# P6 of the feed-forward residual by leaves in the first two blocks, and an engine order picked from 800 plans

## The chip, the cores and the metric

The kernel runs on one core of one Trainium2 chip. The metric is the device time of one execution in microseconds (us); lower is better. Before the change the median of three runs is 566.54 us (566.49 to 567.19).

## The reference

The input is x of 2 x 2048 rows of 512 float32 numbers, and a condition of 2 x 512. What is computed, cut to what matters here:

```python
emb = jnp.dot(jax.nn.silu(t), ada_w) + ada_b
shift_msa, scale_msa, gate_msa, shift_mlp, scale_mlp, gate_mlp = jnp.split(emb, 6, axis=-1)
norm = _ln(x) * (1.0 + scale_msa[:, None]) + shift_msa[:, None]
h = jax.nn.gelu(jnp.dot(norm, ssm_w1) + ssm_b1, approximate=False)
x = x + gate_msa[:, None] * (jnp.dot(h, ssm_w2) + ssm_b2)
norm2 = _ln(x) * (1.0 + scale_mlp[:, None]) + shift_mlp[:, None]
hf = jax.nn.gelu(jnp.dot(norm2, ff_w1) + ff_b1, approximate=True)
x = x + gate_mlp[:, None] * (jnp.dot(hf, ff_w2) + ff_b2)
```

ssm_w1 and ssm_w2 are 512 x 512, ff_w1 is 512 x 1024 and ff_w2 is 1024 x 512. Everything is float32.

## The kernel before, in words

The 4096 rows are cut into eight blocks of 512 rows. Blocks 0 to 3 belong to the first batch entry, 4 to 7 to the second. First comes the part that the code calls ssm: for each block `norm1`, `ssm1` (the product with ssm_w1 and the gelu), `ssm2` (the product with ssm_w2, gated, added to x) and `norm2`. Then comes the feed-forward part in four steps s of two blocks each: `ff1(s)` makes the hidden layer of two blocks, and `ff2(s, 0)` and `ff2(s, 1)` the two outputs.

**Products by seven parts.** No product is done plainly. Each is split into 2 x 2 quarters and made of seven products of sums (the scheme of Strassen and Winograd; the code calls them P1 to P7). `first` (line 420) and `second` (line 430) make the sums of the quarters by elementwise adds, and the seven products are collected in the accumulating banks of PSUM, in the order that lets one bank carry a partial sum on to the next part. Most products are split twice: a part that is itself made of seven smaller ones is done "by leaves". A leaf has half the columns of a plain part.

**ff2.** For one block, `ff2` (line 1114) forms the operands of the seven outer parts from the hidden layer with `first`, then splits P1, P2, P3, P4, P5 and P7 once more, also with `first`. `chain(r)` for r from 0 to 4 does the leaves of P1, P5 and P7, each in a bank of its own; `parts_of(r)` for r from 0 to 6 does those of P2, P3 and P4 and adds them into the rows of the block; `gather` adds a finished bank to the rows. P6 comes last of the outer parts, and there are two forms of it. `plain_sixth` does it unsplit: 8 matmuls of 256 columns in round 4. `sixth` does it by leaves: 14 matmuls of 128 columns spread over the rounds 0 to 4, with four copies on ScalarE, two adds on GpSimd (POOL) and two adds on VectorE into the bank of P1. Which form is used depends on whether the weights hold leaves for P6 (`by_leaves = "P6" in wops`, line 1179). `fw2_sixth` (line 934) makes these leaves of the weights with four adds of 128 x 256. The main program calls it at the start of the step s = 1 (line 1437), so blocks 0 and 1 use `plain_sixth` and blocks 2 to 7 use `sixth`; for the second batch entry it is called right after the weights are loaded.

**What sets the order.** The code first records every operation in `Plan` (line 21) with its engine or engines, its expected cost and latency, and what it depends on. TensorE's operations run in the order in which they were recorded. For the others, `order` (line 88) sets a latest start for each, counted back from the time at which TensorE is due to need the result, and `simulate` (line 111) plays all engines through and always picks, on each free engine, the most urgent operation that is ready. An elementwise add that has all its operands in SBUF can go to VectorE or to POOL. The simulation also chooses which, and lets only one of the two engines work on such adds at a time. Every DMA but a few goes through SP's queue, and eight are in flight at most. The two rounds of `order` differ only in that the second moves the due times by how late TensorE began at one fixed operation (`anchor`, the first matmul of `ssm1(0)`). The operations are then issued in the order of their planned starts, and each engine keeps that order on the chip and waits by semaphores.

Where the prediction speaks of lines: 256 is `tt`, the elementwise add, subtraction or product of two tensors; 274 an activation; 283 a copy on ScalarE; 294 a matmul; 304 a transpose on TensorE; 316 a DMA; 522 and 523 the statistics of a normalization; 591 the transpose on VectorE in it. The names of tiles are those of SBUF regions that hold several things in turn: `rows` is where ff2 adds up its output (and x in ssm), `hidden` holds the hidden layer, `near` and `far` the sums for ff2, `fw` the weights of ff2, `ring` the loaded parts of ff_w1 and sums for ff1, `turned` the normalized and transposed rows; `bank` is PSUM.

Of the kernel before, what the change touches and what calls it, by code (L numbers as in the profile page):

```python
# [1 line left out]

# [12 lines left out]


class Op:
    __slots__ = ("n", "engs", "fn", "cost", "lat", "shared", "size", "lead", "care", "after", "done", "sooner", "deps", "succ", "late", "on", "start", "end", "note")


class Plan:
# [11 lines left out]
    LITTLE = 1 << 15  # L33
    LANES = 8
    AHEAD, SLACK = 2500.0, 150.0

    def __init__(self, nc):
        self.nc = nc
        self.engines = {"p": nc.tensor, "v": nc.vector, "a": nc.scalar, "g": nc.gpsimd, "s": nc.sync}
        self.ops, self.wrote, self.read, self.known = [], {}, {}, {}  # L40
        self.stage, self.care = "", 0.0
# [44 lines left out]
        return op  # L86

    def order(self):
        ops = self.ops
        for op in ops:  # L90
            if op.engs == "p":
                op.deps = {d for d in op.deps if ops[d].engs != "p"}
            for d in op.deps:
                ops[d].succ.append(op.n)
        t, due = 0.0, {}
        for op in ops:
            if op.engs == "p":
                due[op.n] = t
                t += op.cost["p"]
        for _ in range(2):  # L100
            for op in reversed(ops):
                late = due.get(op.n, 1e9)
                for s in op.succ:
                    late = min(late, ops[s].late - (1 + op.care) * (self.HOP + min(op.lat.values()) + op.size / self.RATE))
                op.late = late - op.sooner
            self.simulate()
            wait = ops[self.anchor].start - due[self.anchor]
            due = {n: t + wait for n, t in due.items()}
        return sorted(ops, key=lambda op: (op.start, op.n))

    def simulate(self):
        ops, hop = self.ops, self.HOP
# [86 lines left out]
def kernel(  # L199
# [51 lines left out]
    def tt(e, o, a, b, f):  # L251
        n, ps = cols(o), in_psum(a, b)
        cost = {"v": n / 0.96 + 70, "g": 2.12 * n + 145}
        plan.add(
            e,
            lambda E: E.tensor_tensor(o, a, b, f),  # L256
            [o],
            [a, b],
            cost,
            {"v": cost["v"] + 85, "g": cost["g"] + 45},  # L260
            "g" if ps else "vg",
        )
# [90 lines left out]
    for n in range(8):  # L353
        t = psum.tile([P, 2 * HT], F32, tag=f"bank{n}", name=f"bank{n}")
# [143 lines left out]
    def gate(g, b, bank):  # L498
        if (g, b) == (2, 0):
            return first_gate(bank)  # L500
        load_row(gate_sb, gates_d[g][b])
        if bank is None:
            return gate_sb
        copy(banks[bank], gate_sb)
        return banks[bank]

    def gate_bias(t, g_ps, row):
        load_row(t, row)
        tt("v", t, g_ps, t, ALU.mult)
        tt("vg", t[:, D // 2 :], t[:, D // 2 :], t[:, : D // 2], ALU.subtract)  # L510
# [364 lines left out]
    def quarter_row(b):  # L875
        t = cut(gb2[b], "p (h e d) -> p h e d", h=2, e=2)
        tt("vg", t[:, :, 1], t[:, :, 1], t[:, :, 0], ALU.subtract)

    def weight2(b, bank):
        plan.stage = f"weight2 {b}"  # L880
        t = w2_t[b]
        load_w(t, w2)
        g = gate(2, b, bank)
        gate_bias(gb2[b], g, b2)
        for k in range(KD):
            tt("v", t[:, k, :], t[:, k, :], g, ALU.mult)
        return second(quarters_of_second(t, KD), thirds(w2_s), cuts=1)
# [45 lines left out]

    def fw2_sixth(plain, leaves):
        leaves["P6"] = leaves_of(plain, 6)

    def weight_fw2(b, bank):
        plan.stage = f"weight_fw2 {b}"
        for n in range(2):
            for o in range(2):  # L940
                dma(fw2_t[:, 4 * n + 2 * o : 4 * n + 2 * o + 2], fw2_source()[n, o], lead=100000.0)
        g = gate(5, b, bank)
        gate_bias(gb5, g, fb2)
        for n in range(2):
# [472 lines left out]
    for i in range(1, NBLK):  # L1417
        if i + 3 < NBLK:
            plan.care = 0.45
            tok[i + 3] = norm1(i + 3)  # L1420
            plan.care = 0.45
        last = i + 2 >= NBLK
        hooks = second_head(i + 1, hid[i + 1]) if last and i + 1 < NBLK else {}
        ssm2(i, hid[i], w2_ops, CARRIED, hooks)
        if i in SOON:
            norm2(i)
        if i == 4:
            ff = weight_fw2(0, 1)
        if i + 1 == PER_B:
            w2_ops = weight2(1, 1)  # L1430
            quarter_row(1)
            w2_leaves[0] = second_leaves(w2_ops)
        if not last:
            hid[i + 2] = ssm1(i + 2, tok[i + 2], w1_ops, second_head(i + 1, hid[i + 1]))
    for s in range(NBLK // 2):
        if s == 1:
            fw2_sixth(*ff)
        if 2 * s == PER_B:
            ff = weight_fw2_loaded(1)
            fw2_sixth(*ff)  # L1440
        if 2 * s + 2 == PER_B:
            weight_fw2_ahead(1)
        ff1(s)
        if 2 * s + 2 < NBLK and 2 * s + 2 not in SOON:
            normed2(2 * s + 2)
        for blk in range(2):
            ff2(s, blk, *ff)
# [51 lines left out]
```

## Time and profile before

| | before |
|---|---|
| median of 3 runs | 566.54 us |
| the profiled execution | 566.59 us |
| its span, first to last instruction | 564.8 us |
| TensorE busy (PE) | 557.8 us, 99% |
| VectorE busy (DVE) | 483.1 us, 86% |
| POOL busy | 379.0 us, 67% |
| ScalarE busy (ACT) | 266.0 us, 47% |
| granted TensorE clock | 1.00 |
| HBM | 209 GB/s over the span |

How to read it: PE is TensorE's matmuls and PEld its weight loads, which run beside them. A matmul of float32 leaves two records in the trace, and a record's time includes the way through the array, so that records overlap: a long row of records is read by the distance of their starts. A group's row ends with the idle time of the engine just before its instructions, and with what ended it. A timeline row is: start, length from the first start to the last end, engine, line, operation, output <- inputs, shape, how many; in brackets the idle time ahead of it and who ended it.

### The profile page before, as it was taken

The numbers are of one execution on the slowest core, as the hardware profiler recorded it, in microseconds if no ns is written. First come the engines' busy times: TensorE is split into PE (matmuls) and PEld (weight loads), VectorE is DVE, ScalarE is ACT, GpSimd is POOL, SyncE is SP. The second block draws the span as 40 slices with busy tenths as digits, with TensorE's granted clock in tenths as the row PEclk, the third lists the DMA queues.
The fourth block names the chain that finished last, engine by engine and source line by source line (L and its number), as shares of the span: only waits on it lengthen the run. The fifth ranks groups of instructions, "written<-read, shape, count | busy, mean of one in ns | idle before, by whom it ended". The sixth has DMA issues, their size and how long they took to land.

```text
span 564.8 us, 10322 instructions
## 1 busy us (share of the span) xinstructions
PE 557.8 (99%) x3553; PEld 506.3 (90%) x3553; DVE 483.1 (86%) x918; ACT 266.0 (47%) x534; POOL 379.0 (67%) x514
## 2 busy tenths in 40 slices
PE   8999999999999999999999999999999999999997
PEld 4888889888898988889999889999889999888997
DVE  5696978888879989898989899999999888789776
ACT  3473856674888845557102347212366122336120
POOL 2887638979826687995547866776776784446660
PEclk9999999999999999999999999999999999999999
DMA  8953799989799879895047899078956041820022
GB/s 315 398 221 87 233 343 308 316 240 320 223 268 369 257 271 273 273 323 185 4 147 255 302 286 332 18 204 282 321 172 198 2 151 46 272 95 28 1 75 74
DMA packets 53057, 119.85 MB, mean 212 GB/s; under 512 B 5473, under 2 KB 10509, under 8 KB 51470
## 3 DMA queue, kind: packets, MB, share of 16 engines
q1 hardware_dynamic: 51842, 118.66, 63.9%
q8 instruction: 28, 0.46, 0.3%
q10 hardware_dynamic: 1164, 0.55, 0.3%
q14 instruction: 23, 0.19, 0.1%
HBM read 77.63 MB, written 40.51 MB: 209 GB/s over the span
## 4 chain that ended last, share of the span: by engine, by line
PE 94%; DVE 3%; DMA 1%; issue 1%; POOL 0%; SPq 0%; DVEq 0%
PE bank L294 94%; DMA fw<-in_L_cond_ada_w_dram 1%; DVE hidden L256 1%; DVE near L256 0%; DVE marks L522 0%; PE bank L304 0%; POOL hidden L256 0%; POOL near L256 0%; SPq L316 0%; DVE rows L256 0%; DVE ring L256 0%; DVE fw L256 0%; DVE far L591 0%; DVE turned L656 0%; DVE marks L523 0%
## 5 line engine op out<-in xcount | busy, mean ns | idle before, releaser
L294 PE MATMUL bank<-turned,ring 128*128 128x256 f32 x896 | 208.7, 380 | 0.2 <-DVE turned L656 0.2
L294 PEld LDWEIGHTS bank<-turned,ring 128*128 128x128 f32 x896 | 167.6, 190 | 22.9 <-DVE turned L656 0.5
L256 DVE TENSOR_TENSOR hidden<-bank,hidden 128x512 f32<-128x512 f32 (+1 forms) x171 | 125.2, 755 | 28.0 <-PE bank L294 24.8
L294 PE MATMUL bank<-near,hidden 128*128 128x256 f32 (+1 forms) x470 | 95.3, 350 | 0.3 <-DVE rows L256 0.2
L294 PEld LDWEIGHTS bank<-near,hidden 128*128 128x128 f32 x470 | 82.1, 190 | 10.0 <-DVE rows L256 0.6
L294 PE MATMUL bank<-fw,hidden 128*128 128x128 f32 x640 | 90.4, 275 | 0.0
L256 DVE TENSOR_TENSOR rows<-bank,rows 128x128 f32<-128x128 f32 (+3 forms) x154 | 78.8, 554 | 11.4 <-PE bank L294 10.9
L294 PE MATMUL bank<-ring 128*128 128x256 f32 x336 | 82.4, 381 | 0.5 <-DVE hidden L256 0.5
L294 PEld LDWEIGHTS bank<-fw,hidden 128*128 128x128 f32 x640 | 81.2, 192 | 0.4
L283 ACT COPY bank<-bank 128x512 f32<-128x512 f32 (+2 forms) x88 | 37.3, 425 | 83.3 <-PE bank L294 82.2
L256 POOL TENSOR_TENSOR turned<-turned 128x512 f32<-128x512 f32 (+1 forms) x56 | 63.1, 1139 | 16.7 <-ACT turned L274 9.4
L294 PEld LDWEIGHTS bank<-ring 128*128 128x128 f32 x336 | 63.2, 190 | 11.2 <-issue 1.7
L294 PE MATMUL bank<-fw,far 128*128 128x128 f32 (+2 forms) x644 | 67.6, 278 | 0.7 <-DMA fw<-in_L_cond_ada_w_dram 0.7
L294 PEld LDWEIGHTS bank<-fw,far 128*128 128x128 f32 (+1 forms) x644 | 60.9, 167 | 2.7 <-issue 1.7
L274 ACT ACTIVATE hidden<-hidden,cols 128x512 f32<-128x512 f32 (+1 forms) x66 | 45.0, 712 | 37.9 <-DVE hidden L256 37.8
L294 PE MATMUL bank<-fw,near 128*128 128x128 f32 (+1 forms) x452 | 61.1, 279 | 0.0
L256 POOL TENSOR_TENSOR hidden<-hidden 128x128 f32<-128x128 f32 (+2 forms) x52 | 43.6, 847 | 22.6 <-DVE hidden L256 6.4
L294 PEld LDWEIGHTS bank<-fw,near 128*128 128x128 f32 x452 | 56.0, 192 | 0.4
L256 POOL TENSOR_TENSOR fw<-fw 128x256 f32<-128x256 f32 (+1 forms) x52 | 45.0, 875 | 13.3 <-DVE fw L256 7.7
L274 ACT ACTIVATE turned<-turned,mod,mod 128x512 f32<-128x512 f32 x56 | 41.5, 805 | 8.2 <-DMA turned<-turned 7.2
L256 POOL TENSOR_TENSOR ring<-turned,ring 128x256 f32<-128x256 f32 x37 | 27.8, 757 | 15.8 <-PE bank L294 9.7
L256 DVE TENSOR_TENSOR hidden<-hidden 128x512 f32<-128x512 f32 (+2 forms) x58 | 34.9, 621 | 1.2 <-ACT hidden L274 0.8
(136 smaller groups left out, 692.4 us busy)
## 6 DMA issues: line engine op xcount, KB each, us to landing
ring<-fw_parts SPq DMA_DIRECT2D x28, 512.0 KB
turned<-far SPq DMA_DIRECT2D x52, 256.0 KB
ring<-fw_parts SPq DMA_DIRECT2D x28, 384.0 KB
rows<-x SPq DMA_DIRECT2D x32, 256.0 KB
turned<-turned SPq DMA_DIRECT2D x32, 256.0 KB
out_dram<-rows SPq DMA_DIRECT2D x28, 256.0 KB
fw_parts<-fw SPq DMA_DIRECT2D x21, 256.0 KB
fw<-in_L_cond_ada_w_dram SPq DMA_DIRECT2D x5, 1024.0 KB
```

Of the source, the lines that this page charges most:

```text
L256: lambda E: E.tensor_tensor(o, a, b, f),
L274: lambda E: E.activation(o, a, func, bias=bias, scale=scale),
L283: plan.add("a", lambda E: E.copy(o, a), [o], [a], {"a": cost}, {"a": cost + 60})
L294: lambda E: E.matmul(o, lhsT, rhs, start=start, stop=stop, skip_group_check=True, **kw),
```

## The change

Two things change. First, `fw2_sixth` is called right after `weight_fw2(0, 1)` (after block 4 of ssm2), not at s = 1. So the weights hold P6's leaves from the start, and blocks 0 and 1 use `sixth` as the others do.

Second, `order` no longer takes the one plan. It draws up 800 more with a fixed seed. Each takes the last accepted plan, picks a gap of over 30 ns that TensorE has in it (the longer, the likelier), goes back from an operation that the gap waited for over a few of its predecessors, and asks for that operation earlier by 0.5 to 3 times the gap (`wanted`). `draw_up` sets the latest starts with these wishes and runs `simulate`. The plan's cost is then the end of TensorE in `follow`, which plays the order that came out, unchanged, in three cases: with 700 ns to land for a transfer at the full rate, with 2200 ns, and with 1200 ns at 0.85 of the rate. A plan that costs a little more is accepted too, less and less so; the cheapest of all is issued.

```diff
-        t, due = 0.0, {}
-        for op in ops:
-            if op.engs == "p":
-                due[op.n] = t
-                t += op.cost["p"]
-        for _ in range(2):
-            for op in reversed(ops):
-                late = due.get(op.n, 1e9)
-                for s in op.succ:
-                    late = min(late, ops[s].late - (1 + op.care) * (self.HOP + min(op.lat.values()) + op.size / self.RATE))
-                op.late = late - op.sooner
-            self.simulate()
-            wait = ops[self.anchor].start - due[self.anchor]
-            due = {n: t + wait for n, t in due.items()}
-        return sorted(ops, key=lambda op: (op.start, op.n))
+        tensor = [op for op in ops if op.engs == "p"]
...
+        draw = random.Random(2)
+        wanted, (cost, gaps) = {}, self.draw_up({})
+        best = cost, wanted
+        for n in range(self.ROUNDS):
+            other = dict(wanted)
+            if other and draw.random() < 0.3:
+                del other[draw.choice(list(other))]
+            for d, over in draw.choices(gaps, [g[0] for g in gaps])[0][1]:
+                for _ in range(draw.choice((0, 0, 1, 2, 3, 5, 8))):
+                    before = [u for u in ops[d].deps if ops[u].engs != "p"]
+                    if not before:
+                        break
+                    d = max(before, key=lambda u: ops[u].end)
+                other[d] = other.get(d, 0.0) + over * draw.choice((0.5, 1.0, 1.5, 3.0))
+            found = self.draw_up(other)
+            if found[0] <= cost + draw.random() * self.WARMTH * (1 - n / self.ROUNDS):
+                wanted, (cost, gaps) = other, found
+                if cost < best[0]:
+                    best = cost, wanted
+        self.draw_up(best[1])
+        return self.sequence
...
+    def follow(self, landing, pace, gaps):
...
+        for op in self.sequence:
...
+            if e == "p" and start > free[e] + self.LEAST and op.n > self.anchor:
+                gaps.append((start - free[e], [(d, end[d] + hop - free[e]) for d in op.deps if end[d] + hop > free[e]]))
+            free[e] = start + op.cost[e]
+        return free["p"]
...
         if i == 4:
             ff = weight_fw2(0, 1)
+            fw2_sixth(*ff)
...
     for s in range(NBLK // 2):
-        if s == 1:
-            fw2_sixth(*ff)
         if 2 * s == PER_B:
```

More of the change, by code (lines that the diff above doesn't have):

```diff
@@ L1 @@
+import random
 from contextlib import ExitStack
@@ L17 @@
 class Op:
-    __slots__ = ("n", "engs", "fn", "cost", "lat", "shared", "size", "lead", "care", "after", "done", "sooner", "deps", "succ", "late", "on", "start", "end", "note")
+    __slots__ = ("n", "engs", "fn", "cost", "lat", "shared", "size", "lead", "care", "after", "done", "sooner", "deps", "succ", "due", "late", "on", "start", "end", "note")
 class Plan:
@@ L35 @@
     AHEAD, SLACK = 2500.0, 150.0
+    ROUNDS, WARMTH, LEAST = 800, 300.0, 30.0
+    CASES = ((700.0, 1.0), (2200.0, 1.0), (1200.0, 0.85))
     def __init__(self, nc):
@@ L109, in order @@
-        return sorted(ops, key=lambda op: (op.start, op.n))
+        tensor = [op for op in ops if op.engs == "p"]
+        t = 0.0
+        for op in tensor:
+            op.due, t = t, t + op.cost["p"]
+        self.draw_up({})
+        wait = ops[self.anchor].start - ops[self.anchor].due
+        for op in tensor:
+            op.due += wait
+        draw = random.Random(2)
[17 more added lines that the diff above has]
+                    best = cost, wanted
@@ new lines, in order, with draw_up @@
+        self.draw_up(best[1])
+        return self.sequence
+    def draw_up(self, wanted):
+        ops = self.ops
+        for op in reversed(ops):
+            late = op.due if op.engs == "p" else 1e9
+            for s in op.succ:
+                late = min(late, ops[s].late - (1 + op.care) * (self.HOP + min(op.lat.values()) + op.size / self.RATE))
+            op.late = late - op.sooner - wanted.get(op.n, 0.0)
+        self.simulate()
+        self.sequence = sorted(ops, key=lambda op: (op.start, op.n))
+        cost, gaps = 0.0, []
+        for landing, pace in self.CASES:
+            cost += self.follow(landing, pace, gaps) / len(self.CASES)
+        return cost, gaps
@@ new lines, in follow @@
+    def follow(self, landing, pace, gaps):
+        ops, hop, end = self.ops, self.HOP, [0.0] * len(self.ops)
+        free = dict.fromkeys("pvags", 0.0)
+        pipe, lock, lanes = 0.0, 0.0, [0.0] * self.LANES
+        for op in self.sequence:
+            e = op.on
+            ready = 0.0
+            for d in op.deps:
+                t = end[d] if ops[d].on == e and not ops[d].size else end[d] + hop
+                if t > ready:
+                    ready = t
+            start = max(free[e], ready)
+            if op.size:
+                start = max(start, lanes[0])
+                pipe = max(start + self.FLIGHT, pipe) + op.size / (self.RATE * pace)
+                end[op.n] = (pipe if op.size > self.LITTLE else start + op.lat[e]) + landing
+                lanes = lanes[1:] + [end[op.n]]
+            else:
+                if e in op.shared:
+                    start = max(start, lock)
+                    lock = start + op.cost[e]
+                end[op.n] = start + op.lat[e]
+            if e == "p" and start > free[e] + self.LEAST and op.n > self.anchor:
+                gaps.append((start - free[e], [(d, end[d] + hop - free[e]) for d in op.deps if end[d] + hop > free[e]]))
+            free[e] = start + op.cost[e]
+        return free["p"]
```

## The prediction

> **What bounds the kernel now.** I read the page's first and fourth parts, then the busy times by stage, then the chain of waits, and last the timeline at each place where TensorE stands still.
>
> ```profile
> span 564.8 us, 10322 instructions
> ...
> PE 557.8 (99%) x3553; PEld 506.3 (90%) x3553; DVE 483.1 (86%) x918; ACT 266.0 (47%) x534; POOL 379.0 (67%) x514
> ...
> PE 94%; DVE 3%; DMA 1%; issue 1%; POOL 0%; SPq 0%; DVEq 0%
> ```
>
> TensorE is busy for 557.8 of 564.8 us and makes up 94% of the chain, so only two things can shorten the run: less work on TensorE, and the few waits that are left. The profiled execution took 566.59 us, 1.8 more than its span and 0.05 more than the median of the three runs (566.54).
>
> ```profile
> core 0: us, PE busy (x) PEld busy (x) DVE busy (x) ACT busy (x) POOL busy (x), PEclk, DMA share, GB/s
> ...
> 33.10:208.17 175.07, 174.81 (x989) 155.69 (x989) 147.01 (x307) 120.45 (x243) 123.96 (x214) 1.00 0.82 265
> ...
> 255.36:342.68 87.32, 87.08 (x565) 80.68 (x565) 79.13 (x141) 28.95 (x59) 57.07 (x60) 1.00 0.60 204
> 342.68:429.34 86.66, 86.65 (x588) 80.84 (x589) 81.64 (x144) 34.89 (x73) 61.86 (x68) 1.00 0.64 209
> 429.34:515.91 86.57, 86.56 (x588) 80.82 (x589) 74.13 (x130) 29.47 (x64) 51.96 (x56) 1.00 0.38 119
> ```
>
> The columns are the stretch, its length, and what each engine is busy of it. I cut at the end of each feed-forward up-projection (ff1), so each of the last three rows holds two blocks of ff2 and the next ff1. The second row is blocks 0 and 1, which do P6 plainly; the third is blocks 2 and 3, which do it by leaves, and it is 0.66 us shorter. The first row, the bulk of ssm, has TensorE busy for all but 0.26 us. The granted clock is 1.00 in all, so no throttle enters the sum.
>
> **Part 1: P6 by leaves in blocks 0 and 1.** Per block, `plain_sixth` is 8 matmuls of 256 columns, and `sixth` is 14 of 128. A float32 matmul leaves two records here: the two groups below hold 2 blocks x 8 matmuls in 32 records. Behind them stands the timeline of narrow ones.
>
> ```profile
> L294 PE MATMUL bank<-fw,near 128*128 128x256 f32 x16 | 3.6, 379 | 0.0
> L294 PE MATMUL bank<-fw,far 128*128 128x256 f32 x16 | 3.6, 379 | 0.0
> ```
>
> ```profile
> 384.26 1.06 PE L294 MATMUL bank<-fw,hidden 128*128 128x128 f32 x8
> 385.15 0.61 PE L294 MATMUL bank<-fw,far 128*128 128x128 f32 x4
> 385.60 1.27 PE L294 MATMUL bank<-fw,hidden 128*128 128x128 f32 x8
> ```
>
> Records overlap, so the spacing counts. Sixteen wide ones take 3.6 us and the last is 0.38 long: (3.6 - 0.38) / 15 = 0.215. Eight narrow ones run from 384.26 to 385.15: 0.111 to 0.112. So 16 x 0.216 = 3.46 us becomes 28 x 0.112 = 3.14: 0.32 less per block, **-0.64** for two. The stretches agree: 0.66 apart, with almost the same waits in both.
>
> The other instructions of this part lie beside TensorE. Per block there are three adds of 128x256 for the leaves, one subtraction, four copies on ScalarE (29 of 87 us busy), two small adds on POOL and two adds into the bank on VectorE. At 0.41 us an add that is at most 3.7 us more on VectorE in that stretch (nine such adds, four or five per block). VectorE then has 82.8 of about 86.7 us, hardly more than the 81.6 of 86.66 that blocks 2 and 3 show with the same work. The four adds that make P6's leaves of the weights leave ff2 1 and go into `weight_fw2 0`, where one of them is on POOL. They lie in the first row's stretch, where TensorE hardly waits, so I cost them at nothing; if that cover went, their price would be 4 x 0.41 = 1.6 at most.
>
> **Part 2: the order.** TensorE keeps its order; what moves is VectorE, POOL, ScalarE and SP between 26 us and the end. So I go from one stop of TensorE to the next, with the instruction order of both programs beside it.
>
> The stop at 207.9 us (last block of ssm2):
>
> ```profile
> 203.45 4.48 PE L294 MATMUL bank<-near,hidden 128*128 128x256 f32 x20
> ...
> 206.86 0.68 DVE L591 STREAM_TRANSPOSE far<-near 128x512 f32<-128x512 f32 x1
> ...
> 207.46 0.65 DVE L256 TENSOR_TENSOR rows<-bank,rows 128x512 f32<-128x512 f32 x1
> ...
> 208.17 1.35 PE L294 MATMUL bank<-near,hidden 128*128 128x256 f32 x5 [0.24 <-DVE rows L256]
> ```
>
> Twenty records at 0.216 make the next due at 207.77; it starts at 208.17, 0.40 late, and the five records then take 1.35 instead of 4 x 0.216 + 0.38 = 1.24, so 0.10 is lost in starting again: 0.50 in all. It waits for the `rows` add, which stands behind a transpose that nobody needs yet. In the new order this add stands ahead of that transpose. It then starts at 206.86 and ends at 207.51, 0.26 before it is needed: **-0.50**. Late next is the transpose, by one add; only the normalization of a later block waits for it. The `rows` add after it moves ahead of a transpose as well, so no stop takes the place of this one.
>
> The stops at the ends of ff1 0 and ff1 1:
>
> ```profile
> 252.80 2.32 PE L294 MATMUL bank<-turned,ring 128*128 128x256 f32 x10
> 255.36 1.10 PE L294 MATMUL bank<-ring 128*128 128x256 f32 x4 [0.24 <-DVE hidden L256]
> ...
> 339.68 2.75 PE L294 MATMUL bank<-turned,ring 128*128 128x256 f32 x12
> 342.68 1.10 PE L294 MATMUL bank<-ring 128*128 128x256 f32 x4 [0.24 <-DVE hidden L256]
> ...
> 426.56 2.77 PE L294 MATMUL bank<-turned,ring 128*128 128x256 f32 x12
> 429.34 1.10 PE L294 MATMUL bank<-ring 128*128 128x256 f32 x4
> ```
>
> By the same reckoning the first is due at 254.96 and comes at 255.36 (0.40 late, 0.07 for the new start), the second is 0.41 + 0.07 late, but the third, the end of ff1 2, only 0.19 + 0.07. The arithmetic is the same in all three. In the first two the last adds on VectorE stand as wide (128x1024), narrow (128x512), narrow, wide, narrow, and TensorE waits for the last. In ff1 2 one narrow add stands elsewhere: wide, narrow, wide, narrow. The new order has this form in ff1 0 and ff1 1 too. So each goes from 0.47 to about 0.26: **-0.44** in all. What stays is the last narrow add itself, which waits for the matmul ahead of it.
>
> A new stop, early in block 1 of ff2. In the old order the adds that make P7 and its leaves for block 1 stand before ff2 0's last two wide adds on VectorE; in the new one two adds of 128x512 and the 128x256 add that needs them stand behind the second wide one.
>
> ```profile
> 278.06 1.06 PE L294 MATMUL bank<-fw,hidden 128*128 128x128 f32 x8
> ...
> 278.21 1.23 DVE L256 TENSOR_TENSOR rows<-bank,rows 128x1024 f32<-128x1024 f32 x1
> ```
>
> The three adds as groups of that stretch (busy, mean ns of one), and two neighbours on the timeline:
>
> ```profile
> L256 DVE TENSOR_TENSOR near<-near 128x512 f32<-128x512 f32 x3 | 2.1, 684 | 0.1
> L256 DVE TENSOR_TENSOR fw<-fw 128x256 f32<-128x256 f32 x3 | 1.2, 411 | 0.0
> ```
>
> ```profile
> 255.13 0.68 DVE L256 TENSOR_TENSOR near<-near 128x512 f32<-128x512 f32 x1
> 255.73 0.69 DVE L256 TENSOR_TENSOR hidden<-hidden 128x512 f32<-128x512 f32 x1
> ```
>
> On the old clock the wide add starts at 278.21. End to end the four take 1.23 + 0.68 + 0.68 + 0.41 = 3.00. Neighbours overlap by 0.08 (the two rows at 255), so 2.76 is the least, and 0.2 for the step between an add and one that needs it is the most that I allow over 3.00. So the leaf is ready between 280.97 and 281.4. TensorE gets there after 24 narrow records from 278.06, at 280.75. The wait is 0.2 to 0.65, with 0.1 for the new start: **+0.3 to +0.75, and I take +0.5**, because POOL holds the same two-input adds there. It is the price of a plan that puts three leaf adds more on this stretch.
>
> At 28 us two gating products of weight2 change places on VectorE, so TensorE can be held one step earlier.
>
> ```profile
> 30.54 1.29 POOL hidden L256
> 31.83 1.25 POOL near L256
> 33.08 0.04 issue
> 33.12 3.72 PE bank L294 x16
> ```
>
> The chain of waits above (start, length, what) shows that this costs nothing: TensorE starts at 33.12 because a POOL chain ends then, and that chain stays as it was.
>
> One more stop is lost time of another kind: in the row at 385.60 eight records take 1.27 where eight took 1.06, so 0.21 is lost. VectorE was late, and these rows of VectorE and POOL show why:
>
> ```profile
> 382.86 2.04 DVE L256 TENSOR_TENSOR turned<-turned 128x512 f32<-128x512 f32 x2
> ```
>
> ```profile
> 276.44 0.74 POOL L256 TENSOR_TENSOR far<-hidden 128x256 f32<-128x256 f32 x1 [3.76 <-issue]
> 277.14 1.28 POOL L256 TENSOR_TENSOR far<-far 128x512 f32<-128x512 f32 x1
> ```
>
> Two such adds take about 1.28 undisturbed; here 2.04, so one stood still for 0.76. The work around it is reordered between VectorE and POOL, so this stop may go or stay: between 0 and -0.21, I take **-0.10**.
>
> The queue of SP changes too: from 133 us on loads and stores change places. I cost that at nothing:
>
> ```profile
> PE bank L294 <- DMA fw<-in_L_cond_ada_w_dram: 0.7, 2, 0.4
> ```
>
> This is the only DMA for which TensorE waits (us in total, times, longest), in the first 11 us, and the transfers lie beside matmuls at a share of 0.60 to 0.82. If that cover went, a load of 384 KB of ff1's weights that comes one transfer too late would cost 0.38 MB / 209 GB/s = 1.9 us, which the upper end of the range almost holds.
>
> Sum: -0.64 - 0.50 - 0.44 + 0.5 - 0.10 = -1.18 against the profiled 566.59: 565.4. Against the median that is 566.54 - 1.2 = **565.3**.
>
> The Trainium skill ("SBUF — State Buffer", section "SBUF: two separate sides") says that VectorE with two SBUF inputs and GpSimd share one port pair under an exclusive lock, and that the loser stands still for the whole instruction. The row at 382.86 agrees with it. By that rule a plan that fits to 0.1 or 0.2 us is worth less than its figures, since a POOL add of 1.28 can fall ahead of any VectorE add; that is the first rival.
>
> **The rivals.**
> 1. Collisions take back what the order gains. At the places where the new order leaves VectorE little in hand (the ends of the four ff1, the start of block 1, the first ff1 after ssm2), one collision of 0.76 costs TensorE about 0.4 after what is in hand. Two more than before: 565.3 + 0.8 = 566.1. For it: 385.60 already shows one, and POOL's 57 us in blocks 0 and 1 rise by about one. Against it: before has one such loss in four stretches.
> 2. The order doesn't do what it says: VectorE is 91% busy in that stretch, so an add that goes ahead pushes another, and the waits only change places. Then the leaves' -0.64 and the new +0.5 remain: 566.4. Against it: the stretch of blocks 2 and 3 shows the shorter end of ff1 at even more VectorE work.
> 3. Slower: VectorE becomes the bound of the stretch of blocks 0 and 1. TensorE needs about 86.2 us there (86.66 less waits of about 0.5). VectorE has 79.1 busy and idles 8.2; the change adds up to 3.7, which leaves 4.5 in hand. From the sixth collision of 0.76 on (4.5 us), each lengthens the run by its 0.76; nine to ten in all give 565.3 + 3.4 x 0.76 = 567.9. For it: nine adds more on VectorE in one stretch. Against it: blocks 2 and 3 do the same work in 86.66.
> 4. Better: the new stop stays at its lower end (0.3) and the loss at 385.60 goes with its whole 0.21, while a part of the stops that stay (0.26 at each end of ff1, four of them) is hidden: 564.8.
>
> **How the numbers follow.** Forecast 0.48 (its own range 564.9 to 565.8), rival 1 0.13, rival 2 0.05, rival 3 0.12, rival 4 0.22. A measurement of this kernel can tell about 0.2% (1.13 us) from no change, so faster means under 565.41. The forecast lies nearly on that line: 0.27 of its 0.48 go to the faster side, and with rival 4 that is 0.49. Same: 0.21 + 0.13 + 0.05 = 0.39. Slower: 0.12. The range reaches from 564.5 (past rival 4) to 566.9 (past rivals 1 and 2, short of rival 3), which leaves out rival 3 and the edges, under 2 in 10.
>
> **What would show it.** In the changed profile: no records of 128x256 with `fw,near` and `fw,far`, and 56 records of 128x128 more in their place; no wait of TensorE for `rows` near 207; ends of ff1 0 and ff1 1 that lose about 0.26 like ff1 2; a stop of 0.3 to 0.75 some 25 us after the end of ff1 0; the stretch of blocks 0 and 1 at about 87.0. Wrong would be: a stop in a place named nowhere here, a TensorE wait for a DMA after 33 us (the moves on SP), or VectorE idle under 1 us in blocks 0 and 1.

## The result, and the profile after

| | before | after |
|---|---|---|
| median | 566.56 us (8 runs, 566.49 to 567.19) | 567.98 us (8 runs, 567.61 to 569.12) |
| the profiled execution | 566.59 us | 568.18 us |
| first product of `ssm1` starts at | 14.07 us | 15.35 us |
| last record of TensorE starts at | 560.60 us | 562.20 us |

The ratio is 1.0026, with an interval of 1.0018 to 1.0035: slower by 1.4 us, where 1.2 us less was forecast. (One slip ahead of the prediction: `by_leaves` stands in line 1149 of the kernel before, not in 1179.) All line numbers of the profile rise by 61: 256 is now 317, 294 is 355, 304 is 365, 1354 is 1415.

The first lines of the page of the changed kernel, and its stretches (columns as in the prediction: stretch, length, busy us of PE, PEld, VectorE, ScalarE and POOL, then the clock), cut again at the end of each ff1:

```profile
span 566.4 us, 10409 instructions
...
PE 559.0 (99%) x3577; PEld 506.8 (89%) x3577; DVE 485.1 (86%) x924; ACT 267.4 (47%) x542; POOL 384.2 (68%) x524
```

```profile
34.40:209.47 175.07, 175.07 (x993) 156.26 (x992) 144.13 (x303) 119.75 (x242) 126.90 (x219) 1.00 0.82 263
256.02:343.13 87.11, 86.82 (x589) 80.94 (x589) 81.60 (x141) 33.89 (x71) 63.29 (x67) 1.00 0.57 190
343.13:430.69 87.56, 87.20 (x588) 81.03 (x589) 82.55 (x150) 32.08 (x68) 61.27 (x68) 1.00 0.66 223
430.69:517.52 86.83, 86.70 (x589) 80.77 (x589) 75.36 (x132) 29.40 (x64) 50.16 (x55) 1.00 0.36 119
```

Blocks 0 and 1 take 87.11 us in place of 87.32, so little of the leaves' gain is left there; blocks 2 and 3 take 0.90 more than before (87.56 for 86.66) though their own work did not change; and POOL has 63.29 us of work in blocks 0 and 1 where it had 57.07. The clock is 1.00 throughout.

I measured each stop again as the time over the spacing of records (0.112 and 0.216). What the prediction named came nearly as it said. The stop at 207.9 is gone, and the two ends of ff1 lose 0.25 each where they lost 0.48:

```profile
206.68 3.19 PE L355 MATMUL bank<-near,hidden 128*128 128x256 f32 x14
...
208.15 0.67 DVE L317 TENSOR_TENSOR rows<-bank,rows 128x512 f32<-128x512 f32 x1
...
208.74 0.70 DVE L652 STREAM_TRANSPOSE far<-near 128x512 f32<-128x512 f32 x1
...
253.64 2.36 PE L355 MATMUL bank<-turned,ring 128*128 128x256 f32 x10
...
256.01 0.89 PE L355 MATMUL bank<-ring 128*128 128x256 f32 x3
```

(14 records at 0.216 with 0.38 for the last make 3.19: no wait in the row. 10 from 253.64 make the next due at 255.80; it comes at 256.01.) The new stop early in block 1 is there too, and the three adds stand as foretold behind the wide one:

```profile
278.52 1.23 DVE L317 TENSOR_TENSOR rows<-bank,rows 128x1024 f32<-128x1024 f32 x1
...
279.66 1.45 DVE L317 TENSOR_TENSOR hidden<-hidden 128x512 f32<-128x512 f32 x2
...
281.15 0.42 DVE L317 TENSOR_TENSOR far<-hidden 128x256 f32<-128x256 f32 x1
...
281.62 0.60 PE L355 MATMUL bank<-fw,far 128*128 128x128 f32 x3 [0.28 <-DVE far L317]
```

What the prediction did not name is at three places. First the start. The timeline of the kernel before:

```profile
1.35 5.98 PE L294 MATMUL bank<-far 128*128 128x512 f32 x8 [1.35 <-POOL small L321]
7.30 0.23 PE L304 MATMUL bank<-far,fw 44*128 44x44 f32 x1
7.57 0.20 DVE L1354 COPY cols<-bank 128x44 f32<-128x44 f32 x1 [0.32 <-PE bank L304]
...
11.17 1.09 PE L304 MATMUL bank<-far 128*128 128x128 f32 x8
...
14.07 2.21 PE L294 MATMUL bank<-turned,ring 128*128 128x256 f32 x9 [0.21 <-DVE turned L656]
```

and of the changed one:

```profile
1.34 6.73 PE L355 MATMUL bank<-far 128*128 128x512 f32 x8 [1.34 <-POOL small L382]
8.00 0.26 PE L365 MATMUL bank<-far,fw 44*128 44x44 f32 x1
8.30 0.20 DVE L1415 COPY cols<-bank 128x44 f32<-128x44 f32 x1 [2.48 <-PE bank L365]
...
12.29 1.25 PE L365 MATMUL bank<-far 128*128 128x128 f32 x8 [1.10 <-DVE far L642]
...
15.35 0.92 PE L355 MATMUL bank<-turned,ring 128*128 128x256 f32 x3 [0.21 <-DVE turned L717]
```

The copy `cols<-bank` needs a small transpose of TensorE. In the old order it stands behind three of the normalization's four statistics and waits 0.32 us; in the new one it stands behind the first only, and VectorE idles 2.48 us with three to do behind it. The transposes of x then wait 1.10 for the normalized rows.

Second, early in block 2, in front of the matmuls at 346.27 and 347.07, TensorE loses 0.42 + 0.10 and 0.25 + 0.10 (the lateness and the new start), together 0.88:

```profile
342.79 1.26 POOL L317 TENSOR_TENSOR near<-hidden,near 128x512 f32<-128x512 f32 x1
342.90 1.71 DVE L317 TENSOR_TENSOR far<-near,far 128x512 f32<-128x512 f32 x1
...
344.53 0.68 DVE L317 TENSOR_TENSOR near<-near 128x512 f32<-128x512 f32 x1
345.13 1.28 DVE L317 TENSOR_TENSOR hidden<-bank,hidden 128x512 f32<-128x512 f32 x2
...
346.27 0.71 PE L355 MATMUL bank<-fw,hidden 128*128 128x128 f32 x4 [0.26 <-ACT bank L344]
```

VectorE's add takes 1.71 beside a POOL add, where the next one takes 0.68, and everything behind it is late. Third, at 515 a loss of 0.28 + 0.10 = 0.39 behind an add that began late for no reason in the rows (below).

The account, in us against the kernel before: leaves -0.64, the stop at 207.9 -0.50, ends of ff1 -0.46, the stop at 386 gone -0.21; the start +1.28, block 1 +0.62, block 2 +0.88, 515 +0.39, and +0.10 at 369: +1.46 of the 1.59 by which the profiled executions differ (0.12 at 216 is most of the rest).

### The profile page after: what moved, and what is told of

It is laid out like the page before. It is cut to its first block, busy times and chain, and to the rows that moved or that the text cites. A ratio compares the mean times of both kernels' runs of the same rounds, so it can differ in the third digit from the quotient of the medians.

```text
span 566.4 us, 10409 instructions
## 1 busy us (share of the span) xinstructions
PE 559.0 (99%) x3577; PEld 506.8 (89%) x3577; DVE 485.1 (86%) x924; ACT 267.4 (47%) x542; POOL 384.2 (68%) x524
## 4 chain that ended last, share of the span: by engine, by line
PE 95%; DVE 3%; POOL 0%; issue 0%; DVEq 0%; POOLq 0%
PE bank L355 95%; DVE rows L317 1%; DVE hidden L317 1%; PE bank L365 1%; DVE far L317 1%; DVE fw L317 0%; POOL hidden L317 0%; DVE marks L583 0%; DVE near L317 0%; DVE bank L317 0%; POOL marks L617 0%; DVE far L642 0%; DVE turned L717 0%; DVE bank L542 0%; POOL far masks.py:199 0%
## 5 line engine op out<-in xcount | busy, mean ns | idle before, releaser
L317 POOL TENSOR_TENSOR turned<-turned 128x512 f32<-128x512 f32 (+1 forms) x60 | 67.3, 1134 | 17.5 <-ACT turned L335 9.2
L317 POOL TENSOR_TENSOR hidden<-hidden 128x512 f32<-128x512 f32 (+2 forms) x56 | 49.1, 885 | 28.1 <-DVE hidden L317 14.0
L355 PE MATMUL bank<-fw,far 128*128 128x128 f32 (+1 forms) x656 | 67.7, 276 | 0.3 <-DVE far L317 0.3
L355 PE MATMUL bank<-fw,near 128*128 128x128 f32 x464 | 61.1, 275 | 0.1
L317 POOL TENSOR_TENSOR fw<-fw 128x256 f32<-128x256 f32 (+1 forms) x54 | 47.0, 879 | 9.2 <-DVE fw L317 8.3
L335 ACT ACTIVATE hidden<-bank,cols 128x256 f32<-128x256 f32 x62 | 26.6, 472 | 16.0 <-PE bank L355 15.7
```

Of the source, the lines that this page charges most:

```text
L335: lambda E: E.activation(o, a, func, bias=bias, scale=scale),
L355: lambda E: E.matmul(o, lhsT, rhs, start=start, stop=stop, skip_group_check=True, **kw),
```

## The experiments

All but two of these kernels (the leaves alone, and part 2 alone) carry the order that the planner drew up as a fixed list, so that only what is named moves. In the edits of the changed kernel the line numbers are then 425 (adds), 463 (matmuls), 452 (copies). Each was timed beside the kernel before, which took 566.50 to 566.52 on four chips. An interval reaches about 0.1% (0.5 us) to either side of a ratio, so smaller steps from one kernel to the next rest on the stops in their profiles.

### The start: one copy

```diff
 VectorE, changed kernel: statistics 1 of 4, aggregate,
-copy cols<-bank,
 statistics 2 and 3, aggregates,
+copy cols<-bank,
 statistics 4, ...
```

> The changed kernel's order, with one instruction put back: the copy cols<-bank stands behind the statistics on VectorE again, as in the kernel before. Theory 1 (the copy, waiting for TensorE's transpose at 8 us, holds up the statistics, and the first product starts 1.28 us later): 568.0 - 1.28 = 566.7, first matmul from turned,ring near 14.1. Theory 2 (the start differs from run to run only, and collisions of VectorE and POOL made the kernel slower): 568.0, first matmul near 15.3 or scattered.

Measured: 566.90 (566.74 to 567.43), 1.08 less than the changed kernel; first product at 14.02. Against the kernel before, the ratio is 1.0007 (0.9999 to 1.0016), so without this copy the change is still no gain.

```diff
 VectorE, kernel before: statistics 1 of 4, aggregate,
+copy cols<-bank,
 statistics 2 and 3, aggregates,
-copy cols<-bank,
 statistics 4, ...
```

> The kernel before, with only this copy moved ahead of the second pair of statistics on VectorE, as the new order has it. Theory 1: 566.55 + 1.28 = 567.8. Theory 2: 566.55.

Measured: 567.50 (566.93 to 567.81), ratio 1.0016 (1.0007 to 1.0025): 0.98 more than the kernel before. Theory 1 holds from both sides, at about 1.0, and the profile of this kernel shows the same picture:

```profile
7.97 0.26 PE L469 MATMUL bank<-far,fw 44*128 44x44 f32 x1
8.27 0.20 DVE L1519 COPY cols<-bank 128x44 f32<-128x44 f32 x1 [2.56 <-PE bank L469]
...
15.32 0.92 PE L459 MATMUL bank<-turned,ring 128*128 128x256 f32 x3 [0.21 <-DVE turned L821]
```

Why 1.0 in the medians and 1.28 in the profile: TensorE's first four matmuls (eight records of 128x512) take 5.21 to 6.73 us from profile to profile, with the same order on TensorE, and the small transpose comes between 6.97 and 8.00. With the copy late, the first product starts between 13.96 and 14.09 in the profiles of twelve kernels, whenever the transpose came (7.29 to 7.88). With the copy early, VectorE waits for it, and the run takes over the scatter; in the run on the plans alone (below) TensorE happened to be early. With the rows stand the weight loads (PEld) that run beside its sixth and seventh record:

```profile
1.34 5.70 PE L355 MATMUL bank<-far 128*128 128x512 f32 x8 [1.34 <-POOL small L382]
...
5.59 0.19 PEld L355 LDWEIGHTS bank<-far 128*128 128x128 f32 x1 [0.34 <-issue]
...
6.02 0.19 PEld L355 LDWEIGHTS bank<-far 128*128 128x128 f32 x1 [0.24 <-issue]
...
6.97 0.26 PE L365 MATMUL bank<-far,fw 44*128 44x44 f32 x1
7.27 0.20 DVE L1415 COPY cols<-bank 128x44 f32<-128x44 f32 x1 [1.58 <-PE bank L365]
...
14.32 1.99 PE L355 MATMUL bank<-turned,ring 128*128 128x256 f32 x8 [0.21 <-DVE turned L717]
```

The Trainium skill ("TensorE: Matmul & The Clock Gate", section "Part 1: The HAM clock gate (the "warmup" mystery)") says that the window after which TensorE's clock rises runs freely, so that the rise shifts by up to 0.5 us either way. The granted clock in the rows reads 1.00 from the first microsecond, but the distance of the records shows a change of pace: they start 0.85 us apart at first and 0.43 later. Here the change shifts by more than the page says: it falls between 4.07 and 4.67 in the run with the leaf adds first (below), between 4.92 and 5.59 in the run on the plans alone, and in the changed kernel not before the last of the eight, at 7.48. That is where the scatter comes from.

This is also why the planner does not see what the copy costs there. It counts 853 ns for a matmul of 512 columns (line 288 before, 349 after), both records together, which is the later pace; at the early pace it is 0.85 us a record. So the four matmuls are 3.41 us to it, and in the changed kernel's profile the transpose comes 6.66 us behind the first of them: most of the wait of 2.48 does not exist in the plan.

### The leaves alone

```diff
             ff = weight_fw2(0, 1)
+            fw2_sixth(*ff)
...
-        if s == 1:
-            fw2_sixth(*ff)
```

> Part 1 alone: P6 by leaves in blocks 0 and 1, with the order that the kernel before draws up for it (one plan). Theory A (the prediction's first term, the adds lie beside TensorE): 566.55 - 0.64 = 565.9, or up to 566.5 with a stop of 0.5 in block 1. Theory B (the adds for the leaves find no room on VectorE and POOL between 255 and 282 us, so they come out on TensorE): nine adds of 0.34 to 0.41 unhidden give up to 3.1 to 3.7, so 567.5 to 569, with TensorE waiting for far or hidden sums of VectorE or POOL around 280 us.

Measured: 569.85 (569.03 to 570.03), ratio 1.0055 (1.0042 to 1.0067): theory B, 3.3 slower in the median. Three of the five runs have a granted clock of 0.996 to 0.997 and took 569.85 or more; the two at 0.999 and 1.00 took 569.03 and 569.17, which is 2.5 to 2.7 slower. In the profile (569.03) TensorE loses 3.1 between 278 and 283.3 us, and 3.1 less the leaves' 0.64 is 2.5:

```profile
277.51 1.06 PE L294 MATMUL bank<-fw,hidden 128*128 128x128 f32 x8
...
280.36 1.94 PE L294 MATMUL bank<-fw,far 128*128 128x128 f32 x12 [1.79 <-POOL far L256]
...
283.20 1.05 PE L294 MATMUL bank<-fw,far 128*128 128x128 f32 x7 [0.29 <-DVE far L256]
```

So the leaves are no gain on their own. TensorE's 0.64 is real, but the adds that it takes find no room there, and in the changed kernel, with part 2, the 3.1 are 0.62. A part of the work there is adds of 128x256 on the weights. Between the end of ff1 0 and 285 us VectorE has three of them, 1.2 us in all, in the kernel before (POOL three more), and this group in the changed one (POOL one); two of the six make P6's leaves:

```profile
L317 DVE TENSOR_TENSOR fw<-fw 128x256 f32<-128x256 f32 x6 | 3.2, 551 | 0.0
```

### The three stops alone

```diff
 VectorE, kernel before: ...
+add rows<-bank,rows, add rows<-bank,rows (each ahead of the transpose that it stood behind)
 ff1 0 and ff1 1:
-wide, narrow, narrow, wide, narrow
+narrow, wide, narrow, wide, narrow
```

> The kernel before with three edits of VectorE's order alone: the rows add goes ahead of the transpose at 206.9, the next one ahead of the transpose behind it, and one narrow add of ff1 0 and of ff1 1 goes ahead of the wide ones. Theory A (each stop's size is what the prediction gives it): 566.55 - 0.50 - 0.44 = 565.6. Theory B (an add that goes ahead pushes another, so waits only change places): 566.5.

Measured: 565.78 (565.72 to 565.93), ratio 0.9987 (0.9978 to 0.9995). The stop at 207.9 is gone and the ends of ff1 show 0.25 each, as in theory A; 0.23 comes back as a new stop in ff1 1 at 339.5, where my narrow add stands too early. Theory B is out for two of the three stops; for the third, 0.23 of what the edit won only changed its place.

### The stop in block 2

```diff
 VectorE: ...
+add far<-near,far  (before the add at 330.5)
...
-add far<-near,far  (342.9)
```

> The kernel with the copy late (566.9), and one more instruction moved: VectorE's add far<-near,far, which took 1.71 us beside a POOL add at 342.9, goes to a place 12 us earlier. Theory P (this collision alone makes the two stops of 0.87 at 345.7 and 346.7): 566.9 - 0.87 = 566.0. Theory Q (POOL itself is about 1.1 us late there, after an unbroken row of adds from 327 us, so the sum near<-near that needs POOL's last add is late with or without the collision): 566.8 to 567.0, the stops stay within 0.2 of their size.

Measured: 566.92 (566.84 to 567.46), as without the edit (566.90). Theory Q: the collision is gone, and the stops are as long as before, since the sum that VectorE adds up next waits for POOL anyway:

```profile
341.96 1.27 POOL L425 TENSOR_TENSOR near<-hidden,near 128x512 f32<-128x512 f32 x1
...
343.26 0.69 DVE L425 TENSOR_TENSOR near<-near 128x512 f32<-128x512 f32 x1 [1.53 <-POOL near L425]
...
345.01 0.71 PE L463 MATMUL bank<-fw,hidden 128*128 128x128 f32 x4 [0.26 <-ACT bank L452]
```

```diff
-POOL: add far<-far 128x512 (332.0)
+VectorE: the same add (330.5)
```

> The kernel with the copy late (566.9), and one add far<-far of 128x512 moved from POOL's unbroken row (at 332 us, 1.28 us long) to VectorE, into its idle time at 330.5. Theory Q (POOL's lateness is the cause): the stops at 345.7 and 346.7 go, 566.9 - 0.87 = 566.0. Theory P (only the place of VectorE's own add counts, it stays where it is): at best half of it, 566.5.

Measured: 565.85 (565.72 to 566.09), ratio 0.9988 (0.9979 to 0.9997), 1.05 less. In its profile the two stops come to 0.27 in place of 0.88 (-0.61), though VectorE still collides (1.09 for its add): theory Q for the most part. The 0.39 at 515 is gone as well (VectorE has one instruction more ahead of it, see below), which explains the rest:

```profile
340.85 1.28 POOL L425 TENSOR_TENSOR near<-hidden,near 128x512 f32<-128x512 f32 x1
...
341.57 1.09 DVE L425 TENSOR_TENSOR far<-near,far 128x512 f32<-128x512 f32 x1
...
344.52 0.61 PE L463 MATMUL bank<-fw,hidden 128*128 128x128 f32 x4
```

The row of POOL ended 1.1 us earlier by one add of 1.28 less. The collision that I had first seen was a companion, not the cause. Nor did such collisions become more: of VectorE's adds within SBUF, 19 of 128x512 took over 0.95 us in the kernel before and 19 in the changed one, and of those of 128x256 32 and 30 took over 0.6. The Trainium skill ("SBUF — State Buffer", section "SBUF: two separate sides") has the loser of the shared port wait for the whole instruction, and the 1.71 at 342.9 agrees; by that rule alone the run with this add moved should have gained.

### The stop in block 1

```diff
-POOL: weight add fw<-fw 128x512 (270.7)
+VectorE: the same add
```

> As the run with one POOL add on VectorE, and a second one: the weight add fw<-fw of 128x512 at 270.7 us goes from POOL to VectorE (0.68 there in place of 1.27 of the shared port). Theory (the stop at 280.7 to 281.6 is port time that the leaves' adds need there): it shrinks from 0.62 to 0.3 or less, 565.4 to 565.7. Rival (the stop is set by the order of VectorE's own queue behind the wide add): it stays or grows by the 0.6 that VectorE does more, 566.0 to 566.6.

Measured: 565.62 (565.52 to 566.03), ratio 0.9985 (0.9975 to 0.9994). The stop goes from 0.62 to 0.43: the direction of the theory, less than its size.

```diff
 VectorE: ...
+add, add, leaf add (block 1, P7)
 wide add into rows
-add, add, leaf add
```

> The kernel with two adds on VectorE (565.62), and the three adds of block 1's P7 and its leaf moved ahead of the second wide add into rows, as the kernel before has them. Theory order (the prediction's reading: the stop at 280 us is these adds' place behind the wide add): the 0.43 that is left goes, 565.2. Theory room (VectorE is full from 268 to 282 us, so whatever stands last is late): the wide add comes 1.8 us later, ScalarE's copy bank<-small and TensorE wait for it, 566.5 to 567.8.

Measured: 569.07 (567.42 to 569.28), ratio 1.0040 (1.0026 to 1.0054). Three of the five runs lie at 569.07 to 569.28 with a granted clock of 0.996 to 0.997, two at 567.42 and 567.60 with 0.999 and 1.00; 0.3% of 567 is 1.7, about the distance between them. Why the clock was lower in the three stays open. The profiled run is the one of 567.42, in the range of theory room:

```profile
276.88 2.51 DVE L425 TENSOR_TENSOR hidden<-hidden 128x512 f32<-128x512 f32 x2
...
281.08 0.38 ACT L452 COPY bank<-small 128x256 f32<-128x256 f32 x1 [3.85 <-DVE rows L425]
...
281.51 0.71 PE L463 MATMUL bank<-fw,hidden 128*128 128x128 f32 x4 [1.89 <-ACT bank L452]
```

With the leaf adds first, the wide add is late, and with it the copy that clears a bank. VectorE has no room there (13.45 of 14.00 us busy from 268 to 282 us in the changed kernel): what stands last is late.

```diff
 VectorE, with the two adds of POOL:
+add hidden<-hidden (block 1, P7)
 narrow add, narrow add, wide add into rows
-add hidden<-hidden
-POOL: add far<-far,hidden 128x256 (block 1)
+VectorE: the same add
```

> The kernel with two adds on VectorE (565.62), with one of block 1's adds of 128x512 ahead of two adds into rows, and one add of 128x256 moved from POOL to VectorE. If the rest of the stop at 280 us is room, spreading the work takes 0.1 to 0.3 off: 565.3 to 565.5. If not: 565.6 or more.

Measured: 565.88 (565.78 to 566.20), no gain. The stop at 280 us went from 0.43 to 0.07, with 0.20 at 276 in its place, but the 0.39 came back at 512.7, and 0.21 at 471.

### An order for all of it

```diff
-POOL: 519 instructions
+POOL: 485 instructions, 405 of them in the old order
-VectorE: 924
+VectorE: 958, 792 of them in the old order
```

> All the operations of the changed kernel with an order of VectorE and POOL that leaves POOL room: 34 adds moved from POOL to VectorE, about one in eight of both engines' instructions at another place, TensorE, ScalarE and the transfers in the order of the changed kernel. If both theories (the early copy, POOL late in unbroken rows) name most of what was lost, only the four ends of ff1 (0.25 each) and the start remain: 564.0 to 564.8, below the kernel before by 0.3 to 0.45%. If the losses were of another kind (collisions that come at random whatever the order): 566 or more.

Measured: 567.53 (567.00 to 569.29), ratio 1.0022 (1.0011 to 1.0032): a miss. The stops at 280 and 345 are gone, and new ones stand at 214 (0.36), 307 (0.34), 316 (0.62) and 340 (0.53). At 316:

```profile
312.72 1.52 DVE L425 TENSOR_TENSOR ring<-turned,ring 128x256 f32<-128x256 f32 x1
...
315.36 1.04 DVE L425 TENSOR_TENSOR rows<-rows,near 128x512 f32<-128x512 f32 x1
...
317.06 1.13 PE L463 MATMUL bank<-turned,ring 128*128 128x256 f32 x4 [0.35 <-DVE hidden L425]
```

An add that takes 0.41 alone took 1.52, one of 0.68 took 1.04. An order that was made for the stops that I knew made others. The run moved too much at once to tell what each of these comes from.

### Part 2 alone

```diff
 changed kernel:
-            fw2_sixth(*ff)     (after weight_fw2)
...
+        if s == 1:
+            fw2_sixth(*ff)
```

> Part 2 alone: the operations of the kernel before (P6 plain in blocks 0 and 1) with the order picked from 800 plans. This plan, too, has the copy cols<-bank early. By the prediction's terms for part 2 (-0.50 - 0.44 - 0.10): 565.5 without a price for the copy, 566.5 with the 1.05 that the two runs on the copy gave. Rival (the new order makes POOL late in further places): over 566.8.

Measured: 567.17 (566.48 to 568.09), ratio 1.0010 (1.0001 to 1.0019): on the rival's side, and part 2 alone is no gain either.

```diff
 VectorE, the same, but:
-copy cols<-bank behind statistics 1
+copy cols<-bank behind statistics 3
```

> Part 2 alone (P6 plain in blocks 0 and 1, the order picked from 800 plans), with the copy cols<-bank back behind the statistics. By the prediction's terms for part 2: 565.5. Rival (the order fits its plan to 0.1 us, and POOL that comes later than planned makes new stops): 566.0 to 567, with stops of 0.3 to 0.9 in ff1 or early in ff2 that the kernel before hasn't.

Measured: 566.27 (566.14 to 566.35), ratio 0.9995 (0.9986 to 1.0005): the rival. The copy costs 0.90 here. Without it the plans give 0.2 of the 1.04 that I had counted, which the interval does not tell from nothing: the stop at 207.9 is gone and the two ends of ff1 are down to 0.25, but a stop of 0.37 at 426 is new, and the one at 515 has grown from 0.25 to 0.66. Whether POOL makes these two, as the rival has it, no run tells.

### The stop at 515

In the changed kernel VectorE stood idle at 514.3:

```profile
511.11 3.15 DVE L317 TENSOR_TENSOR hidden<-bank,hidden 128x1024 f32<-128x1024 f32 x3
514.76 1.82 DVE L317 TENSOR_TENSOR hidden<-bank,hidden 128x512 f32<-128x512 f32 x2 [0.50 <-PE bank L355]
```

The row names TensorE, but that matmul had ended at 513.66, and VectorE's wait instruction at 514.35; the add began 0.41 after that. The same add did so in three kernels; in the leaves alone another one did (396.0 us), and in the run with one more add on VectorE a third (510.5). Counted from 0 in VectorE's records, waits among them, all are number 1087 or 831, which is 63 more than a multiple of 128, and all stand right behind a wait. The only transfer near 515 is a load of instructions, and it begins at 515.71, after the add.

```diff
-POOL: add turned<-turned 128x256 (481)
+VectorE: the same add, in an idle place (484.6)
```

> The kernel with the copy late (566.9), and one add turned<-turned of 128x256 moved from POOL (481 us) to VectorE, where it stands idle for 1 us at 484.6. Nothing near 515 changes but the count of VectorE's instructions. Theory K (the delay of 0.41 belongs to the count 128n + 63 behind a wait of its own): the stop at 513.7 goes, 566.9 - 0.39 = 566.5. Theory L (it belongs to this add, its bank or its neighbours on POOL): it stays, 566.9.

Measured: 566.45 (566.36 to 566.93), 0.45 less: theory K. With one instruction more ahead of it the six adds run without a gap, while POOL's adds beside them keep their places:

```profile
509.71 5.89 DVE L425 TENSOR_TENSOR hidden<-bank,hidden 128x1024 f32<-128x1024 f32 x6
```

It isn't a full rule: in the kernel before, number 703 (5 x 128 + 63) is also an add behind a wait, and lost nothing. What delays the add stays open. The loading of instructions does not explain it as recorded: in the leaves alone the nearest load of that queue begins 4 us after the late add, and in this run it stands at 512.12 and nothing is late.

### The version that beats both

```diff
 the changed kernel, copy cols<-bank late,
-POOL: far<-far (332.0), fw<-fw (270.7)
+VectorE: the same two
 VectorE, block 1:
+add hidden<-hidden ahead of two narrow adds into rows
```

> The kernel with two adds on VectorE (565.62), and only one of block 1's adds of 128x512 ahead of two adds into rows. Theory room (the leaf adds of block 1 lack VectorE time, and a little is won where a waiting place is filled): the stop of 0.43 at 279.6 shrinks to about 0.2, 565.4, and the stop at 513 stays away, since VectorE's count of instructions stays. Theory order: 565.2.

Measured: 565.42 (565.36 to 565.51), ratio 0.9980 (0.9971 to 0.9989): 1.1 below the kernel before, 2.6 below the changed one. 0.08 is left at 280 (ten records at 0.112 with 0.275 for the last make 1.28), with 0.20 at 276:

```profile
279.91 1.36 PE L463 MATMUL bank<-fw,far 128*128 128x128 f32 x10
```

## Why the prediction was wrong

- **"What moves is VectorE, POOL, ScalarE and SP between 26 us and the end"**: this step failed, with the largest price. The instruction order of VectorE differs from 4 us on. The copy had moved ahead of three statistics, and costs 0.90 to 1.08 by three pairs of runs (1.28 in the profiles). The working went from one stop of the kernel before to the next, and its first 15 us hold none that the change removes; what the new order does there was left out. It is not the whole miss: with the copy late the time is 566.90, and the forecast was 565.3. The stops in block 2 (0.88) and at 515 (0.39) make up most of the rest.
- **POOL's work "rises by about one"** (rival 1, chance 0.13): this step failed too. It rose by 6.2 in blocks 0 and 1 (57.07 to 63.29), while VectorE, for which nine adds more were reckoned, has 141 instructions there in both kernels. The place of the rival was right, the ends of ff1 and what follows, and its price of 0.4 for each of two collisions is near the 0.88 of block 2; that is luck, for the mechanism was POOL's lateness: taking the collision away changed nothing (566.92 for 566.90), taking one add from POOL took 0.61 off.
- **Part 1, -0.64**: right on TensorE (24 records more by the page, 56 of 0.112 for 32 of 0.216), and no record of 128x256 with `fw` is left. "The other instructions lie beside TensorE" is wrong: alone, with one plan, they cost 3.1, so 2.5 net at the full clock. "The four adds ... lie in the first row's stretch" is wrong for three of the four: one is at 192.9, the others at 243.4, 261.6 and 268.1 us, the last two where VectorE is full.
- **The stop at 207.9, -0.50**: right. **The ends of ff1, -0.44**: right (-0.46). Both stops also go, or shrink to 0.25, when the three edits are done alone, with 0.23 lost again at 339.5.
- **The new stop in block 1, +0.5 (0.3 to 0.75)**: right in place and size (0.62). Its reason was half right: the adds do stand behind the wide one, but to put them ahead costs 1.8 and more, so it is room more than order. One weight add less on POOL took it to 0.43, one add of block 1 further ahead to 0.28 in two places.
- **385.6, -0.10**: it went with its whole 0.21. **Weight2, SP at nothing**: right, TensorE waits for no transfer after 26 us.
- Named nowhere: the 0.39 at 515, of a kind that costs nothing in the trace of before, and small stops at 216 and 369.
- **Rival 3**, the only one that has the kernel slower, was wrong in its mechanism: VectorE has 81.60 of 87.11 us, and idles 5.5.

## What to carry to other kernels

Compare the order of every engine over the whole program, the start above all: an instruction that waits for another engine and has moved forward holds up everything behind it, and a planner that counts the other engine as faster than it is there will not tell. Where a stop follows a collision of two engines, ask first whether the other engine's row of work, here unbroken for 15 us, would be late without it: in block 2, taking an add from that row took most of the stop away, and moving the colliding add took nothing. More of the same is not safe: 34 adds fewer on POOL made the kernel slower. A plan that fits to 0.1 us gains what it removes and can lose it again at other places: the same plan with four moves by hand won 1.1 us where it had lost 1.4.

## What the runs showed of the hardware

- VectorE can begin an add 0.41 us late at a certain count of its instructions (number 1087 or 831 of its records, 63 more than a multiple of 128) behind a wait; one instruction more ahead of it removed 0.39 at 515 (566.90 to 566.45 in the medians). Number 703 behind a wait lost nothing, and the cause stays open.
- TensorE's first four matmuls of 128x512 took 5.21 to 6.73 us from kernel to kernel, though TensorE's order is the same there: their records start 0.85 us apart until a moment that differs from run to run (from 4.1 to past 7.4 us), and 0.43 from then on. It costs nothing while nobody waits for the transpose behind them.
- VectorE adds beside POOL adds took 1.04 to 1.71 where they take 0.41 to 0.68 alone, and a POOL add took 1.73 in place of 1.28 (at 329.4 in the run with one VectorE add earlier): either side can be the one that waits.
